# Two fused attention and feed-forward layers: softmax totals from a column of ones, intermediate results by tokens, later loads held back, more zero matmuls at the start

## The chip, the cores and the metric

The kernel runs on one core of a Trainium2 chip. The metric is the device time of one execution in microseconds (us), as the median of several runs; a profiled execution gives the trace beside it.

## What is computed

Two layers, each an attention branch `s` and a feed-forward branch `g` on the same layer-normalised input, joined as `x + s * silu(g)`. There are 4 batches of 1024 tokens, 128 features, all in float32.

```python
x = L0_attn_x                                   # (4, 1024, 128)
xn = layernorm(x)
s = L0_attn(xn)      # 16 heads of 8, window of 64 tokens back, ALiBi bias, softmax
g = silu(L0_ffn(xn)) # weights mixed from 8 experts, one mixture for each batch
x = x + s * g
xn = layernorm(x)
s = L1_attn(xn)      # attention over the 4 "batches" for each position, gated bias, Wo, bo
g = silu(L1_ffn(xn)) # silu(w1 x) * (w2 x), gelu(h1 .), gelu(h2 .), w3
return x + s * g
```

In the first attention the softmax divides each head's weighted values by the sum of its exponentials:

```python
score = jnp.einsum('bhqd,bhkd->bhqk', q, k) / scale + bias[None]
score = jnp.where(mask[None, None], score, -jnp.inf)
attn = jax.nn.softmax(score, axis=-1)
out = jnp.einsum('bhqk,bhkd->bhqd', attn, v)
```

## The kernel before

**Units and tiles.** A unit is 512 tokens of one batch, so there are 8 units, two to a batch. In the first attention a unit has 4 tiles of 128 queries. The second attention goes by 8 slices of 128 positions over all 4 batches, named by words with a star. Features lie on the partitions and tokens along the free axis nearly everywhere ("by features"); "by tokens" means the transpose of that.

**Order.** PE, DVE and ACT each run their queue in the order in which the program issues it (`manual_schedule`), and that order is written out as a string of words, `ORDER`: a letter for the step, a digit for the unit or batch and mostly one for the part. `s21` is the scores of unit 2, tile 1. The words name: l/n/k the layernorm before the first layer (statistics, scaling, transposing back), t the statistics of the middle one (its n and k have part 1), q the projections, m and v masked queries and values, s scores, b bias added, x exponential, o weighted values and totals, d division, A B C D the gate of the experts, E one expert added into the mixed weights (16 a batch), f and g the first feed-forward, r the residual on POOL, w h i j the second feed-forward. POOL and SP aren't held to the string; their instructions are placed by what they depend on, and each runs in order too.

**Scores and totals.** `scores` (L393) writes a tile's scores into a single PSUM buffer of four banks, `ps_S`; DVE adds the bias from there into SBUF (`biased`, L410), ACT takes the exponential in place (L741). `weighted` then makes, for the tile's 16 heads, the weighted values (L438: 32 products of 64 columns, weights of 32 columns taken from `vb`, which holds values in slots of 24 columns with 8 used) and the totals (L451: 16 products of 128 columns with a matrix of ones, `totals`, or its upper half where a batch's first keys are masked). Both fall into `ps_O`, features on partitions, so that the total stands at each of a head's 8 rows. `divided` (L462, L463) takes the reciprocal of 256 columns for a pair of tiles and multiplies.

**Feed-forward of the first layer.** `hid0` (L472) gives four blocks of hidden features. `out0` (L481) accumulates four products of 512 columns into one bank, mixed weights as the stationary operand, and ACT applies Silu with the bias of each feature (L485). `residual` (L490, L491) multiplies and adds on POOL. The middle layernorm needs tokens on partitions, so `ln_mid` (L224) transposes `x` four times a unit.

**Feed-forward of the second layer and output.** `gated` (L508 to L512), `hidden` (L520, L521; the heaviest group), `out1` (L531, L536, scaled by `w3s` in the Silu at L539). In the second attention's slices `project_out` (L666) is one product of 512 columns, `gated_out` (L672 to L675) adds the bias, multiplies with `g1`, adds `x` and stores. `last_batch` (L687 to L689) stores the last batch.

**Start and loads.** Three products with zeros (L266) run while the first loads come. A bound on the scores is worked out, and the program branches on it to one of two versions; the one with the running maximum left out (`exact` false) is taken. The first unit's expert tables go into buffers of the hidden blocks (`stream_first`, L339), those of later batches through three buffers `tw` (L294), issued when step A of the batch comes. Right after the branch SP issues all other loads: `x` twice (by features and, as `xt` into `g1`, by tokens), the second layer's weights (`load_l1`, L501) and `wa` (L693 to L699).

Of the kernel before, what the change touches and what calls it, by code (L numbers as in the profile page):

```python
# [29 lines left out]
C_ID, C_MP, C_SEL, C_EXP, C_TOT, C_TOF = np.cumsum([0, 128, 4, 64, 256, 128]).tolist()  # L30
C_N = C_TOF + 128
# [3 lines left out]
for _name, _n in (  # L35
    ("gb1", 1), ("gb2", 8), ("b1", 4), ("b2", 1), ("bq", 1), ("bk", 1), ("bv", 1), ("bo", 1),
    ("gW", 8), ("gb", 8), ("ga", 1), ("pb", 4), ("w1s", 4), ("w2s", 4), ("h1s", 4), ("h2s", 4), ("w3s", 1),
):
    VEC[_name] = (sum(n for _, n in VEC.values()), _n)
V_N = sum(n for _, n in VEC.values())  # L40


def constants():
# [13 lines left out]


    tot = np.tile((r[None, :] // 8 == g[:, None]).reshape(1, P), (P, 1))
    c[:, C_TOT:C_TOT + P] = tot  # L60
    c[:, C_TOF:C_TOF + P] = tot * (p[:, None] < W)
# [24 lines left out]

ORDER = """
    l1 n10
    q0 m03 m00 m01 z m02 s00 b00 k10 A00 A01 s01 B0 b01 v00 C0 D0 E0 v01 s02 v03 x01 E0 E0 v02 E0 E0 x00 b02
    o00 s03 E0 x02 E0 l3 E0 E0 b03 o01 E0 f0 d01 E0 f1 E0 x03 E0 f0 f0 E0 E0 f1 E0 l2 o02 o03 n30 f0 d03 n20  # L90
    g0 g0
    q1 v11 k20 k30 r0 t0 f1 m11 A10 n01 m12 g1 k01 v10 f1 v13 w0 m13 g1 m10 v12 w0 w0 s10 A11 b10 w0 s11 x10
    b11 x11 h0 h0 s12 o10 b12 o11 s13 b13 h0
    q2 d11 x12 h0 o12 B1 x13 C1 D1 E1 E1 E1 E1 i0 E1 o13 E1 d13 i0 E1 E1 i0 E1 E1 r1 i0 E1 E1 t1 E1 f2 E1 j0
    v20 v23 j0 f2 f2 E1 m21 m20 E1 n11 g2 v21 f2 k11 m22 g2 v22 w1 m23 w1 s20 w1 b20 w1 h1 l4 x20 h1 s21 n40
    o20 b21 x21 h1 o21 s22 d21 b22 h1 x22 l5 i1 i1 s23 b23 o22 x23 n50 i1 i1 o23 j1 j1 k50 f3 d23
    q3 r2 t2 m31 n21 f3 k40 f3 v31 f3 g3 m30 A20 k21 v32 v33 g3 w2 v30 w2 m32 m33 w2 A21 s30 b30 w2 x30 B2
    h2 s31 o30 b31 C2 x31 h2 s32 o31 D2 h2 E2 b32 h2 x32 E2 i2 d31 i2 E2 o32 E2 E2 E2 s33 E2 E2 b33 E2 x33
    E2 i2 E2 i2 E2 o33 E2 d33
    q4 f4 r3 E2 E2 m43 E2 f4 j2 v40 t3 n31 f4 m41 f4 j2 g4 k31 v42 m40 v43 g4 w3 w3 m42 l6 v41 w3 w3 s40 b40  # L100
    n60 h3 x40 h3 s41 b41 o40 k60 l7 n70 h3 x41 h3 k70 s42 o41 b42 i3 f5 i3 s43 b43 d41 x43 x42 i3 i3 o42
    o43 j3 d43 j3 r4
    q5 t4 f5 m53 f5 n41 A30 m51 m50 f5 v51 g5 k41 g5 v53 w4 m52 v52 v50 w4 w4 s50 b50 w4 x50 A31 h4 h4 B3
    o50 s51 b51 C3 x51 h4 D3 E3 E3 E3 s52 b52 E3 E3 E3 E3 o51 x52 h4 i4 d51 s53 b53 E3 E3 E3 E3 o52 x53 i4
    i4 E3 i4 o53 d53 E3 r5 j4 f6 E3 E3
    q6 f6 t5 m61 E3 f6 m63 f6 n51 v60 j4 v61 g6 k51 g6 v62 w5 m62 v63 w5 m60 w5 w5 s60 b60 h5 x60 h5 s61 o60
    b61 x61 h5 h5 o61 s62 i5 i5 b62 d61 x62 i5 s63 b63 x63 i5 o62 o63 d63 f7 r6 f7 j5 f7 t6 j5 n61 f7
    q7 k61 m71 m70 g7 v70 v73 v71 w6 m72 g7 m73 w6 v72 *A0 w6 s70 *B0 b70 *V0 w6 s71 b71 x70 h6 *A1 *b0 s72
    b72 x71 *C0 *E0 *B1 *N0 x72 o70 h6 *b1 *D0 o71 *A2 d71 *V1 *C1 *B2 o72 s73 *E1 *N1 h6 *G0 b73 *F0 *b2 h6
    *D1 x73 *C2 i6 *E2 o73 i6 *G1 d73 r7 *Y0 *A3 *N2 t7 *V2 *B3 *D2 *b3 n71 *V3 i6 i6 *C3 *E3 *F1 k71 j6 *N3  # L110
    *Y1 w7 *G2 *D3 j6 w7 w7 *A4 *F2 *G3 *F3 *Y2 *Y3 y60 *V5 *B4 *b4 *A5 *A6 w7 *V6 *V4 *C4 *B5 *E4 *b5 *V7
    h7 *B6 *A7 h7 *b6 *N4 *C5 *B7 *b7 *D4 h7 *C7 *E5 h7 *G4 *E7 *F4 *N5 *Y4 *D5 *G5 i7 *C6 *E6 *N6 i7 *F5
    *N7 *D6 *Y5 i7 *D7 *G6 i7 *F6 *G7 j7 *Y6 j7 *F7 y70 *Y7 y71
# [4 lines left out]
def block_kernel(ctx: ExitStack, tc: tile.TileContext, a: dict, out: bass.AP):  # L118
# [20 lines left out]

    x = main.tile([P, B, S], F32, tag="x", name="x")  # L140

    g1 = main.tile([P, B, S], F32, tag="g1", name="g1")
    xt = [g1[:, b, :].rearrange("p (i d) -> p i d", d=P) for b in range(B)]
# [7 lines left out]
    tb = const.tile([P, FC + 1, E], F32, tag="tb", name="tb")  # L151
# [6 lines left out]
    nc.scalar.dma_start(out=g1[:, 0, 0:U], in_=a["xt"][:, 0:U])  # L158
    nc.sync.dma_start(out=wqkv, in_=a["wqkv"])
    nc.sync.dma_start(out=cst, in_=a["const"])  # L160
    nc.scalar.dma_start(out=g1[:, 0, U:S], in_=a["xt"][:, U:S])
# [15 lines left out]
    totals = [cst[:, at:at + P].rearrange("p (g c) -> p g c", g=4) for at in (C_TOT, C_TOF)]  # L177
# [7 lines left out]
    DVE.memset(vb[:, 0:2328], 0.0)  # L185
    POOL.memset(vb[:, 2328:24 + 9 * 512], 0.0)
    slots = vb[:, 24:24 + 9 * 512].rearrange("p (m h q) -> p m h q", m=9, h=H)[:, :, :, 0:HD]

    def tokens(u):

        b, c = u // 2, (u % 2) * U
        return b, slice(c, c + U)

# [21 lines left out]
    def ln_in(u):  # L215

        return ln_stats(xt[u // 2][:, 4 * (u % 2):4 * (u % 2) + 4, :])

    def ln_mid(u):

        b, cx = tokens(u)
        turned = ps.tile([P, 4, P], F32, tag="O", name="ps_T")
        for i in range(4):
            PE.transpose(turned[:, i, :], x[:, b, cx.start + i * P:cx.start + (i + 1) * P], ident)  # L224
        return ln_stats(turned)
# [32 lines left out]

    one = const.tile([P, 1], F32, tag="one", name="one")
    POOL.memset(one, 1.0)  # L260
    in_order = {mybir.EngineType.PE, mybir.EngineType.Activation, mybir.EngineType.DVE}
    with tc.manual_schedule(engines=in_order | {mybir.EngineType.Pool}):
        steps = bound()

        for i in range(3):
            PE.matmul(bank(), lhsT=vb[:, 0:P], rhs=vb[:, 0:U], start=True, stop=True)  # L266
            if i == 1:
                next(steps)
        scale = ln_in(0)
        next(steps)  # L270
        fast = nc.values_load(flag[0:1, 0:1], min_val=0, max_val=1)
        ln_back(0, scale())

    def program(exact):
# [41 lines left out]
        def gates_c(b, gr):  # L316
            shares = small([P, FC + 1, E], "shares")
            DVE.tensor_tensor(shares, tb, gr.unsqueeze(1).to_broadcast([P, FC + 1, E]), ALU.mult)
            mb = at.tile([P, FC + 1], F32, tag="mb", name="mb", bufs=2)
            DVE.tensor_reduce(mb, shares, AX.X, ALU.add)  # L320
            DVE.tensor_tensor(mb, mb, v("b1", 0, FC + 1), ALU.add)
            own = [at.tile([P, F], F32, tag=f"mw{j}", name=f"mw{j}", bufs=2) for j in range(2)]
            mixed[b] = (own[0], own[1], mb)

# [27 lines left out]
        def qkv(u):  # L352
# [26 lines left out]
            def value(i):  # L379
                copy = DVE.tensor_copy if u else ACT.copy  # L380
                rows, first = ((slice(0, W), 0), (slice(0, W), 1), (slice(W, P), 1), (slice(W, P), 2))[i]
                copy(slots[rows, first:first + 7:2], src[rows])
# [45 lines left out]
        def weighted(u, t, pr):  # L428

            if t % 2 == 0:  # L430
                put(("op", u), ps.tile([P, 2, 2 * P], F32, tag="O", name="ps_O"))
            op = made["op", u][:, :, (t % 2) * P:(t % 2) * P + P]
            for i in range(2):
                qs = slice(W * i, W * i + W)
                at0 = 24 + 512 * (2 * t + i)
                for g in range(4):
                    for j in range(4):
                        PE.matmul(  # L438
                            op[32 * j:32 * j + 32, 0, qs],
                            lhsT=vb[:, at0 + 128 * j + 24 * g:at0 + 128 * j + 24 * g + 32],  # L440
                            rhs=pr[:, j, g, qs],
                            start=(g == 0),
                            stop=(g == 3),
                        )
            spans = ((slice(0, P), 0),)
            if u % 2 == 0 and t == 0:
                spans = ((slice(0, W), 1), (slice(W, P), 0))
            for qs, first in spans:
                for g in range(4):
                    for j in range(4):  # L450
                        PE.matmul(  # L451
                            op[32 * j:32 * j + 32, 1, qs],
                            lhsT=totals[first][:, g, :],
                            rhs=pr[:, j, g, qs],
                            start=(g == 0),
                            stop=(g == 3),
                        )

        def divided(t, op, s):

            inv = small([P, 2 * P], "inv")
            DVE.reciprocal(inv, op[:, 1, :])  # L462
            DVE.tensor_tensor(s[:, (t - 1) * P:(t + 1) * P], op[:, 0, :], inv, ALU.mult)  # L463
# [12 lines left out]
        def out0(u, hid):  # L476
            b, _ = tokens(u)
            _, m2, mb = mixed[b]
            op = bank()
            for c in range(FC):  # L480
                PE.matmul(op, lhsT=m2[:, c * P:(c + 1) * P], rhs=hid[:, c, :], start=(c == 0), stop=(c == FC - 1))  # L481
                if c == 1:
                    yield None
            g = tmp.tile([P, U], F32, tag="g", name="g", bufs=1)
            ACT.activation(g, op, AF.Silu, bias=mb[:, FC:FC + 1])  # L485
            yield g

        def residual(u, g, s):
            b, cx = tokens(u)
            POOL.tensor_tensor(g, g, s, ALU.mult)  # L490
            POOL.tensor_tensor(x[:, b, cx], x[:, b, cx], g, ALU.add)  # L491
# [6 lines left out]
        def load_l1():  # L498
# [376 lines left out]
```

## Time and profile before

| what | value |
|---|---|
| median of 3 runs | 586.19 us (586.15 to 586.88) |
| profiled execution, time | 588.99 us |
| profiled execution, span of the core | 587.1 us |
| mean granted TensorE clock | 0.984 |
| loads and stores | 29.35 MB, mean 50 GB/s |
| instruction packets of queue 8 | 46, 0.75 MB |

A profile's line of a group names the line in the kernel, the engine, the operation, the tile written and the tiles read, the shapes and the count; behind the first bar stand the busy time in us and the mean ns of one, behind the second the idle time of the engine just ahead, and what ended it. PE is a matmul, PEld the load of its stationary operand. A product in f32 appears as two passes, a transpose as one, so 32 products are 64 records. Rows of 40 digits are slices of 14.7 us, each digit tenths. In a timeline the columns are start, length, engine, line, operation, tiles, shapes and count, and in square brackets the engine's idle time before it. In a table by stretches each engine has its busy us and its count of instructions, then come granted clock, DMA share and GB/s.

### The profile page before, as it was taken

How to read it: one execution, taken by the hardware profiler on the slowest of the kernel's cores; microseconds unless marked ns; L12 is line 12 of the kernel's file. 1: busy time of each engine (PE TensorE's matmuls, PEld its weight loads, DVE VectorE, ACT ScalarE, POOL GpSimd, SP SyncE). 2: the span in 40 equal slices, each digit the busy share in tenths (PEclk: the TensorE clock that was granted, in tenths of full speed). 3: DMA queues.
4: the chain of work that ended last, by engine and by line, in shares of the span. 5: the costliest groups of instructions: out<-in, count | busy, mean ns of one | idle time of the engine just before them, and what ended most of it. 6: DMA issues, size and time to landing. Idle time of an engine off the chain costs nothing.

```text
span 587.1 us, 12660 instructions
## 1 busy us (share of the span) xinstructions
PE 564.8 (96%) x5608; PEld 287.5 (49%) x5608; DVE 333.9 (57%) x545; ACT 334.2 (57%) x380; POOL 110.6 (19%) x123
## 2 busy tenths in 40 slices
PE   6589999999999999999999999999999999999995
PEld 2356455535455454545554554445554555444443
DVE  5876535755333473663325384743146768878764
ACT  2546757286655736556566564664866747345441
POOL 3012000211002000211010000300021334557433
PEclk8869999999999999999999999999999999999999
DMA  8980000620000012400000032000000000001002
GB/s 306 400 343 2 2 2 3 213 74 2 1 2 0 1 52 95 145 2 1 1 2 1 1 109 73 0 1 2 2 2 1 2 2 11 5 27 33 1 15 64
DMA packets 10750, 29.35 MB, mean 50 GB/s; under 512 B 1216, under 2 KB 4800, under 8 KB 9664
## 3 DMA queue, kind: packets, MB, share of 16 engines
q1 hardware_dynamic: 10256, 26.90, 12.9%
q10 hardware_dynamic: 432, 1.57, 0.7%
q8 instruction: 46, 0.75, 0.5%
q14 instruction: 16, 0.13, 0.1%
HBM read 26.37 MB, written 2.10 MB: 48 GB/s over the span
## 4 chain that ended last, share of the span: by engine, by line
PE 93%; ACT 2%; DMA 1%; DVE 1%; issue 1%; POOL 0%; ACTq 0%; DVEq 0%
PE ps_M L520 38%; PE ps_O L438 6%; PE ps_S L393 6%; PE ps_O L451 5%; PE ps_M L481 5%; PE ps_M L508 4%; PE ps_M L472 4%; PE ps_M L509 4%; PE ps_M L536 4%; PE ps_M L569 4%; PE ps_S L648 1%; PE ps_M L617 1%; PE ps_M L231 1%; PE ps_S L364 1%; PE ps_S L361 1%
## 5 line engine op out<-in xcount | busy, mean ns | idle before, releaser
L520 PE MATMUL ps_M<-big,l1h 128*128 128x512 f32 x512 | 229.6, 598 | 0.0
L520 PEld LDWEIGHTS ps_M<-big,l1h 128*128 128x128 f32 x512 | 94.6, 190 | 115.1 <-issue 110.8
L410 DVE TENSOR_TENSOR big<-ps_S,bias 128x2048 f32<-128x2048 f32 x32 | 73.3, 2290 | 94.9 <-PE ps_S L393 78.0
L521 ACT ACTIVATE big<-ps_M,vec 128x512 f32<-128x512 f32 x64 | 43.9, 687 | 109.1 <-PE ps_M L520 108.7
L741 ACT ACTIVATE big<-big 128x2048 f32<-128x2048 f32 x32 | 61.0, 1910 | 15.4 <-DVE big L410 15.1
L462 DVE RECIPROCAL inv<-ps_O 128x256 f32<-128x256 f32 x16 | 28.1, 1754 | 37.0 <-PE ps_O L451 36.9
L521 ACT ACT_TABLE_LOAD x35 | 44.9, 1283 | 5.6 <-PE ps_M L520 5.0
L490 POOL TENSOR_TENSOR g<-g,s 128x512 f32<-128x512 f32 x8 | 10.8, 1353 | 184.1 <-DVE s L463 179.7
L512 DVE SCALAR_TENSOR_TENSOR big<-ps_M,vec,t2k 128x512 f32<-128x512 f32 x32 | 23.9, 748 | 32.6 <-PE ps_M L509 16.5
L438 PEld LDWEIGHTS ps_O<-big,vb 128*32 128x32 f32 x2048 | 32.3, 114 | 19.6 <-issue 15.0
L438 PE MATMUL ps_O<-big,vb 128*32 128x64 f32 x2048 | 37.5, 226 | 3.9 <-ACT big L741 3.4
L451 PE MATMUL ps_O<-big,cst 128*32 128x128 f32 (+1 forms) x1152 | 36.5, 269 | 3.2 <-issue 3.2
L393 PE MATMUL ps_S<-qm,k 32*64 32x256 f32 (+1 forms) x768 | 36.9, 472 | 2.5 <-DVE big L410 2.5
L330 DVE SCALAR_TENSOR_TENSOR mw<-tw,gr,mw 128x512 f32<-128x512 f32 x42 | 35.1, 836 | 1.2
L741 ACT ACT_TABLE_LOAD x26 | 33.4, 1283 | 3.3 <-DVE big L410 2.9
L508 PE MATMUL ps_M<-xn,l1w 128*128 128x512 f32 x64 | 33.4, 603 | 1.2 <-ACT g L485 1.2
L509 PE MATMUL ps_M<-xn,l1w 128*128 128x512 f32 x64 | 32.9, 595 | 0.0
L473 ACT ACTIVATE big<-ps_M,mb 128x512 f32<-128x512 f32 x32 | 21.7, 687 | 18.8 <-PE ps_M L472 18.5
L511 ACT ACTIVATE t2k<-ps_M,vec 128x512 f32<-128x512 f32 x32 | 22.0, 686 | 17.8 <-PE ps_M L508 17.3
L472 PE MATMUL ps_M<-xn,mw 128*128 128x512 f32 x64 | 31.2, 597 | 0.0
L451 PEld LDWEIGHTS ps_O<-big,cst 128*32 128x32 f32 x1152 | 29.3, 115 | 3.9 <-issue 3.8
L393 PEld LDWEIGHTS ps_S<-qm,k 32*64 32x64 f32 x768 | 18.9, 133 | 24.2 <-issue 11.0
(148 smaller groups left out, 687.0 us busy)
## 6 DMA issues: line engine op xcount, KB each, us to landing
tw<-in_tw SPq DMA_DIRECT2D x24, 512.0 KB, 4.1
big<-in_tw SPq DMA_DIRECT2D x4, 1024.0 KB, 8.2
l1h<-in_l1h SPq DMA_DIRECT2D x2, 1024.0 KB, 15.3
g<-in_xt SPq DMA_DIRECT2D x3, 512.0 KB, 12.1
x<-in_x SPq DMA_DIRECT2D x1, 1536.0 KB, 14.2
out<-t2k SPq DMA_DIRECT2D x8, 192.0 KB, 2.1
bias<-in_bias ACTq DMA_DIRECT2D x1, 1024.0 KB, 7.9
l1w<-in_l1w SPq DMA_DIRECT2D x3, 256.0 KB, 13.9
```

The source lines that it names most:

```text
L330: DVE.scalar_tensor_tensor(m, more[e // 2][:, e % 2, :], gr[:, e:e + 1], base if e == 0 else m, ALU.mult, ALU.add)
L393: PE.matmul(sp[rows, j, :, q0:q0 + n], lhsT=k[r, key:key + W], rhs=qm[r, :, t * P + q0:t * P + q0 + n], start=True, stop=True,)
L410: DVE.tensor_tensor(pr, sp, bias, ALU.add)
L438: PE.matmul(op[32 * j:32 * j + 32, 0, qs], lhsT=vb[:, at0 + 128 * j + 24 * g:at0 + 128 * j + 24 * g + 32], rhs=pr[:, j, g, qs], start=(g = ...
L451: PE.matmul(op[32 * j:32 * j + 32, 1, qs], lhsT=totals[first][:, g, :], rhs=pr[:, j, g, qs], start=(g == 0), stop=(g == 3),)
L472: PE.matmul(hp, lhsT=m1[:, c * P:(c + 1) * P], rhs=xn[:, b, cx], start=True, stop=True)
L481: PE.matmul(op, lhsT=m2[:, c * P:(c + 1) * P], rhs=hid[:, c, :], start=(c == 0), stop=(c == FC - 1))
L508: PE.matmul(p1, lhsT=wt["w1"][:, c * P:(c + 1) * P], rhs=xn[:, b, cx], start=True, stop=True)
L509: PE.matmul(p2, lhsT=wt["w2"][:, c * P:(c + 1) * P], rhs=xn[:, b, cx], start=True, stop=True)
L520: PE.matmul(hp, lhsT=wt[name][:, i, c * P:(c + 1) * P], rhs=hid[:, i, :], start=(i == 0), stop=(i == FC - 1))
L521: ACT.activation(new[:, c, :], hp, AF.Gelu, scale=v(name + "s", c))
L741: ACT.activation(pr, pr, AF.Exp)
```

## The change

1. **Totals.** The slots of `vb` get a ninth column, set to one once; `value` writes only the eight others. `weighted` takes the weights so that each product gives 8 values and the total of a head in 9 neighbouring rows; the three first head groups of a tile fall into one of two parts of `ps_O`, the fourth groups of both tiles share a third part. The second loop with `totals` goes, as do its constants. Where a batch's first keys are masked, the ninth column is zeroed with the rest of the slot.
2. **By tokens.** A new step c copies the pair's result from PSUM on ACT, p transposes its three parts on PE, and d divides by tokens: reciprocals of 24 and 8 columns, and two multiplications. `out0`, `out1` and `project_out` take the hidden block as the stationary operand and the weights as the moving one, four products of 128 columns for each of 512. Biases that lay on partitions are now rows: a new step H (`row_bias`) makes one product for each batch's bias row, DVE adds it ahead of the Silu; `bo` is added by DVE in a step of its own; `w3` is scaled once on POOL by `w3s` (step Z). `x` is loaded, kept and stored by tokens, so that `xt`, the transposes of `ln_mid` and one of two loads of `x` go.
3. **Loads.** `load` (steps L0, L1, L2) sets one column of its target on DVE and then issues the load; the words stand in the first unit's last third. Only `x[1]` is still issued right after the branch.
4. **Start.** Five zero products instead of three, behind a first memset of 512 columns; after the first transposes `row_weights` (two products) and one more zero product of 256 columns.
5. **Order.** The string of words is new throughout. The first unit before:

```
l1 n10 q0 m03 m00 m01 z m02 s00 b00 k10 A00 A01 s01 B0 b01 v00 C0 D0 E0 v01 s02 v03 x01 E0 E0 v02 E0 E0 x00 b02
o00 s03 E0 x02 E0 l3 E0 E0 b03 o01 E0 f0 d01 E0 f1 E0 x03 E0 f0 f0 E0 E0 f1 E0 l2 o02 o03 n30 f0 d03 n20 g0 g0 q1
```

and after:

```
l1 q0 n10 m03 m00 m01 z m02 s00 k10 A00 A01 b00 s01 B0 b01 v00 C0 H0 D0 v01 v03 E0 E0 E0 E0 x01 s02 b02 E0
E0 v02 l3 E0 x00 E0 o00 x02 E0 E0 s03 o01 b03 c01 E0 f1 p01 d01 E0 E0 f0 E0 L0 x03 E0 E0 f0 f0 l2 f1 o02
o03 c03 n30 f0 g0 n20 g0 L1 L2 k30 p03 d03 r0 q1
```

The diff, cut to its core:

```diff
-    DVE.memset(vb[:, 0:2328], 0.0)
+    DVE.memset(vb[:, 0:U], 0.0)
+    DVE.memset(vb[:, U:2328], 0.0)
     POOL.memset(vb[:, 2328:24 + 9 * 512], 0.0)
-    slots = vb[:, 24:24 + 9 * 512].rearrange("p (m h q) -> p m h q", m=9, h=H)[:, :, :, 0:HD]
+    slots = vb[:, 24:24 + 9 * 512].rearrange("p (m h q) -> p m h q", m=9, h=H)[:, :, :, 0:HD + 1]
...
-    def ln_mid(u):
-
-        b, cx = tokens(u)
-        turned = ps.tile([P, 4, P], F32, tag="O", name="ps_T")
-        for i in range(4):
-            PE.transpose(turned[:, i, :], x[:, b, cx.start + i * P:cx.start + (i + 1) * P], ident)
-        return ln_stats(turned)
+    def ln_of(u):
+        return ln_stats(by_tokens(x, u))
...
+    POOL.memset(slots[:, :, :, HD], 1.0)
+    def row_weights():
+
+        rp = bank((P, 4, P))
+        for i in range(2):
+            PE.matmul(rp[:, i, :], lhsT=sb[:, i * P:(i + 1) * P], rhs=sb[:, 2 * P:3 * P], start=True, stop=True)
+        DVE.tensor_scalar(wb[:, 0, :], rp[:, 0, :], 1.0 / S, None, ALU.mult)
+        DVE.tensor_copy(wb[:, 1, :], rp[:, 1, :])
...
-        for i in range(3):
-            PE.matmul(bank(), lhsT=vb[:, 0:P], rhs=vb[:, 0:U], start=True, stop=True)
-            if i == 1:
+        for i in range(5):
+            idle(vb, U)
+            if i == 2:
                 next(steps)
...
         ln_back(0, scale())
+        row_weights()
+        idle(vb, U // 2)
...
+        def row_bias(hrep):
+            rp = bank()
+            PE.matmul(rp[:, 0:D], lhsT=hrep, rhs=wb[:, 0, :], start=True, stop=True)
+            row = at.tile([P, D], F32, tag="row", name="row")
+            DVE.tensor_tensor(row, rp[:, 0:D], wb[:, 1, :], ALU.add)
+            return row
...
             if t % 2 == 0:
-                put(("op", u), ps.tile([P, 2, 2 * P], F32, tag="O", name="ps_O"))
-            op = made["op", u][:, :, (t % 2) * P:(t % 2) * P + P]
+                put(("op", u), ps.tile([P, 3, P], F32, tag="O", name="ps_O"))
+            op, odd = made["op", u], t % 2
             for i in range(2):
                 qs = slice(W * i, W * i + W)
                 at0 = 24 + 512 * (2 * t + i)
                 for g in range(4):
+                    part, row = (odd, 9 * g) if g < 3 else (2, 9 * odd)
                     for j in range(4):
+                        col = at0 + 128 * j + 32 * g - row
                         PE.matmul(
-                            op[32 * j:32 * j + 32, 0, qs],
-                            lhsT=vb[:, at0 + 128 * j + 24 * g:at0 + 128 * j + 24 * g + 32],
+                            op[32 * j:32 * j + 32, part, qs],
+                            lhsT=vb[:, col:col + 32],
                             rhs=pr[:, j, g, qs],
...
-                        PE.matmul(
-                            op[32 * j:32 * j + 32, 1, qs],
-                            lhsT=totals[first][:, g, :],
-                            rhs=pr[:, j, g, qs],
...
-            inv = small([P, 2 * P], "inv")
-            DVE.reciprocal(inv, op[:, 1, :])
-            DVE.tensor_tensor(s[:, (t - 1) * P:(t + 1) * P], op[:, 0, :], inv, ALU.mult)
+        def taken(u, op):
+
+            ab = tmp.tile([P, 3, P], F32, tag="ab", name="ab", bufs=1)
+            ACT.copy(ab, op)
+            return ab
+
+        def turned(ab):
+            tp = bank((P, 4, P))
+            for i in range(3):
+                PE.transpose(tp[:, i, :], ab[:, i, :], ident)
+            return tp
...
+            DVE.reciprocal(i3, most[:, :, :, HD])
+            DVE.reciprocal(i1, rest[:, :, :, HD])
...
-            op = bank()
+            op = bank((P, 4, D))
             for c in range(FC):
-                PE.matmul(op, lhsT=m2[:, c * P:(c + 1) * P], rhs=hid[:, c, :], start=(c == 0), stop=(c == FC - 1))
+                for i in range(4):
+                    PE.matmul(op[:, i, :], lhsT=hid[:, c, i * P:(i + 1) * P], rhs=m2[:, c * D:(c + 1) * D], start=(c + i == 0), stop=(c + i == FC + 2))
...
-            ACT.activation(g, op, AF.Silu, bias=mb[:, FC:FC + 1])
+            DVE.tensor_tensor(g, op, made["row", b].unsqueeze(1).to_broadcast([P, 4, D]), ALU.add)
+            ACT.activation(g, g, AF.Silu)
...
+        def load(*names):
...
+                DVE.memset(to[:, 0:1], 0.0)
+                nc.sync.dma_start(out=to, in_=of)
...
-                op = st["op"] = spare((P, B, L))
-                PE.matmul(op, lhsT=wa[:, 3 * D:4 * D], rhs=xn[:, :, cx], start=True, stop=True)
+                op = st["op"] = spare((P, B, D))
+                for t in range(B):
+                    PE.matmul(op[:, t, :], lhsT=xn[:, t, cx], rhs=wa[:, 3 * D:4 * D], start=True, stop=True)
...
-                DVE.scalar_tensor_tensor(y, op[:, 0:n, :], v("bo"), g1[:, 0:n, cx], ALU.add, ALU.mult)
-                DVE.tensor_scalar(xn[:, n, cx], op[:, n, :], v("bo"), None, ALU.add)
+                DVE.tensor_tensor(xn[:, :, cx], op, v("bo", 0, D).unsqueeze(1).to_broadcast([P, B, D]), ALU.add)
+                DVE.tensor_tensor(y, xn[:, 0:n, cx], g1[:, 0:n, cx], ALU.mult)
...
-        nc.sync.dma_start(out=g1[:, 1, :], in_=a["xt"][:, S:2 * S])
-        nc.sync.dma_start(out=x[:, 0, :], in_=a["x"][:, 0:S])
-        load_l1()
-        for b in range(2, B):
-            nc.sync.dma_start(out=g1[:, b, :], in_=a["xt"][:, b * S:(b + 1) * S])
-        nc.sync.dma_start(out=x[:, 1:B, :].rearrange("p b s -> p (b s)"), in_=a["x"][:, S:B * S])
-        nc.sync.dma_start(out=wa, in_=a["wa"])
+        nc.sync.dma_start(out=x[:, 1, :], in_=a["x"][:, S:2 * S])
...
+            "L": lambda i: load(*(("w1", "w2", "h1"), ("h2", "w3"), ("wa", "x"))[i]), "0": lambda n: idle(cst, P * n), "y": lambda u, i: last_batch(u, i, U if u < 7 else U // 2),
```

## The prediction

> **What bounds the kernel now.** I read the page's first two parts, then a table by stretches, the groups by line, the chain of waits, and the timeline of the first unit and of the end.
>
> ```profile
> PE 564.8 (96%) x5608; PEld 287.5 (49%) x5608; DVE 333.9 (57%) x545; ACT 334.2 (57%) x380; POOL 110.6 (19%) x123
> ...
> PEclk8869999999999999999999999999999999999999
> DMA  8980000620000012400000032000000000001002
> ```
>
> PE is the only engine near its span, and it is short of clock only in the first three slices, where the DMA engines are full. The table by stretches (length, then busy time of PE, PEld, DVE, ACT, POOL, granted clock, DMA share) separates two regimes:
>
> ```profile
> 15.00:30.00 15.00, 9.11 (x184) 5.99 (x186) 12.35 (x20) 8.56 (x13) 1.41 (x4) 0.84 1.00 400
> 30.00:45.00 15.00, 12.14 (x226) 7.61 (x221) 11.32 (x20) 6.67 (x6) 1.95 (x2) 0.71 0.79 319
> ...
> 250.00:300.00 50.00, 50.00 (x548) 25.39 (x551) 20.97 (x39) 33.08 (x35) 3.06 (x6) 1.00 0.01 2
> ```
>
> From about 45 us on, PE works without a gap at full clock, and DVE and ACT are half idle: there a PE pass removed is time removed, and other engines' work is free as long as PE has other work queued. Before 45 us DVE is the fullest queue and PE waits at half clock.
>
> PE's busy time counts overlapping passes twice, so I price passes from start to start. Chain of waits (start, length), then timeline of the second unit:
>
> ```profile
> 143.68 1.03 PE ps_O L438 x64
> 144.71 0.89 PE ps_O L451 x64
> 145.60 3.63 PE ps_M L520 x8
> ```
> ```profile
> 49.32 3.60 PE L481 MATMUL ps_M<-big,mw 128*128 128x512 f32 x8
> ...
> 52.75 1.02 PE L361 MATMUL ps_S<-xn,wqkv 128*128 128x512 f32 x2
> ...
> 54.47 1.05 PE L364 MATMUL ps_S<-wqkv,xn 128*128 128x128 f32 x8
> ...
> 55.36 1.04 PE L231 MATMUL ps_M<-cst,nt 128*128 128x128 f32 x8
> ```
>
> The totals (L451) of one 128-token tile take 0.89 us after its values (L438, 1.03 us). A 512-column f32 product is two passes, (52.75 - 49.32) / 8 = 0.429 us each. A 128-column pass with weights of its own each time is (55.36 - 54.47) / 8 = 0.111 us: four of them are 0.444, so turning a product round into four by tokens costs only 0.015 us a pass.
>
> The first unit, in the timeline: the first bias addition, PE standing in the middle of the totals, and (above) the second unit's queries at 52.75.
>
> ```profile
> 16.96 2.29 DVE L410 TENSOR_TENSOR big<-ps_S,bias 128x2048 f32<-128x2048 f32 x1 [1.31 <-PE ps_S L393]
> ...
> 33.24 0.65 PE L451 MATMUL ps_O<-big,cst 128*32 128x64 f32 x15 [2.47 <-issue]
> ...
> 42.06 4.68 DVE L330 SCALAR_TENSOR_TENSOR mw<-big,gr,mw 128x512 f32<-128x512 f32 x6
> ```
>
> DVE's last expert step ends at 46.74, and DVE sat idle for 30 - 12.35 - 11.32 = 6.3 us between 15 and 45. The 2.47 us wait is for nothing the kernel does[...].
>
> [...]
>
> **The change part by part**, against the profiled execution (span 587.1, 1.9 around it, 589.0 in all; the median of the three runs, 586.2, is 0.5% lower, so a difference in us carries over).
>
> *Totals by a column of ones.* L451 goes. After the first unit that is 28 tiles at 0.89 = -24.9 us (up to 28 if a group followed by another one is worth the 1.0 us that such pairs take). L438 keeps its 32 products a tile, at other addresses: nothing. Added: the result is copied by ACT (16 copies; 582 ns for 512 columns at L232, so about 0.45, 7 us in all, beside PE), turned by three transposes per pair of tiles, and divided by tokens. 42 transposes after the first unit, against 32 that the middle layernorm no longer needs because x now lies by tokens: 10 more at 0.12 = +1.2, and some 7 more changes between tiled and whole array at 0.11 = +0.8. DVE's division falls from 1.75 + 0.42 to about 1.05: from 553 ns for 64 reciprocals (L637) and 1754 for 256 the cost is 0.15 + 0.0063 each, so 0.30 + 0.20, and two small multiplications of 0.35 + 0.2 (256 take 0.42). It is used where DVE waits for PE anyway; free but in the first unit. New is the way o, copy, turn, divide, residual, layernorm: a copy behind an exponential (1.91) and a table load (1.28) on ACT can arrive 3 us late. The order puts other steps between; I take +1.0 in all, bounds -1 (the new order may also remove small gaps: PE is idle 2.3 us between 45 and 575) and +9.
>
> *By tokens.* Passes that were 512 wide: out0 8 in each of 7 later units, out1 8 in each of 7 (the last unit's are halves already), output projection 2 in each of 8 slices: 128 x 0.015 = +1.9. The row bias is two more passes for each of 3 later batches, 0.11 each: +0.7. On DVE 8 additions of 0.69 (a 512-column PSUM read, L372) before the Silu and about 0.35 more per slice in the output step, hidden by PE except in the last slice. DVE's sum falls to about 322 us. w3's scaling is one POOL step of about 1.4 us, long before use.
>
> *Loads held back, fewer bytes.* x no longer comes twice: 2.1 MB less. After the first unit's weights only x[1] and three of the next batch's tables (stream of A10, issued by SP ahead of L0) follow; w1, w2, h1 wait for a DVE memset in the middle of the expert steps, h2, w3, wa and x[2:4] for one after the first output product. So the queues are empty from about 24 us, by (2.6 + 4.2 + 0.5 + 1.6 MB) / 400 GB/s, to 38[...]. SP stands behind those memsets, but what is queued there (the fourth table of batch 1) also waits for a buffer until E1, near 100 us. The loads return as 4.2 MB between 38 and 52 us, when PE has become the bound[...]. Bounds 0 and 2.5 (the stall seen); I take +0.5. w1 is needed about 10 us after its issue and takes 4: hidden.
>
> *More zero matmuls, first unit.* A shorter first memset (512 of 2328 columns, about 0.45 of 2.0 us) lets PE start near 1.8 rather than 3.3, and five zero products instead of three, then the row weights and a half one, fill PE to 11 us; so the projections, 1.65 + 1.71 + 1.18 us at half clock in the chain, should run in about 2.6. The first bias addition then comes at about 15.6 instead of 16.96 (it is held by the four masks on ACT, 2.4 us, and the layernorm before it). From there DVE's queue to the last expert step is 4 x 2.29 + 16 x 0.76 + one layernorm's statistics 1.2 + six small steps 1.2 + a division 1.05 + memsets 0.3 = 25.1, and one wait of about 1 for the second scores (single ps_S buffer): 41.7. PE's products of out0 (32 x 0.111 = 3.6), four transposes and three more (0.8) follow: the second unit's queries start at about 46.2 instead of 52.75, -6.5. Bounds: -8.5 (exponentials earlier) and -3 (clock still lost while PE waits for exponentials near 25 us, with both output groups slow).
>
> *End.* The last slice's output is two DVE steps before POOL instead of one: +0.4.
>
> Sum: -24.9 + 1.2 + 0.8 + 1.0 + 1.9 + 0.7 + 0.5 - 6.5 + 0.4 = -24.9. From the median: 586.2 - 24.9 = **561.3**, said as 561.
>
> **Rivals.** *Loads of weights bind the products by tokens* (slower). 256 + 256 + 64 = 576 passes get weights of 128 columns each. If a pass took as long as its load, 190 ns, that is 576 x 0.079 = +45.5 us: 606. It decides from 0.111 + 24.9 / 576 = 0.154 us a pass. For it: PEld's mean of 190 ns. Against: the eight L364 passes at 111 ns, same shapes.
>
> *The first unit doesn't shorten* and the late loads stall PE once: 561.3 + 5 + 2 = about 568. For it: exponentials and scores through one PSUM buffer still alternate, and PE idles there as before. Against: DVE's own sum above.
>
> *The longer way to the middle layernorm leaves PE without work* for about 1.5 us in each of 7 units: 571. For it: ACT's table loads of 1.28 us and banks in threes. Against: the units are interleaved, and PE's stretches of second-FFN products are 14 us long.
>
> *More is saved*: totals at 1.0 a tile, first unit -8.5, no new waits: 586.2 - 31.5 = 554.7. For it: pairs of tiles at 4.05 us. That the totals aren't really gone is ruled out by the instruction order: no product has the ones matrix any more.
>
> **Numbers.** Forecast 561 (own range 557 to 565): 0.62. More saved: 0.14. First unit not shorter: 0.14. Waits: 0.07. Weight loads: 0.03. From 553 to 569 the first three cases and most of the fourth's lower part lie inside. About 0.2% is what a measurement of this kernel can tell from no change; faster 0.96, same 0.01, slower 0.03.
>
> **What would show it.** Passes of out0 and out1 start 0.11 us apart (0.19: the weight-load rival). Values of a tile, no totals: about 1.0 us to the next group. Queries of the second unit at about 46 us. PE busy in every stretch of 50 us from 50 to 550 at 49 or more; gaps named by ACT's copy or DVE's division would be the third rival. No PE wait named issue before 38 us. The forecast is wrong if PE's gaps after 50 us sum to over 8 us or the second unit starts after 50.

## The result and the profile after

The changed kernel takes 566.87 us (median of 4 runs, 566.34 to 566.92) against 586.27 for the kernel before on the same chip: ratio 0.9665, 95% interval 0.9648 to 0.9682, 19.4 us less. Run again for the experiments, on another chip, it took 566.5 against 588.22: ratio 0.9636 (0.9615 to 0.9657). The kernel before scatters more than the three runs ahead of the prediction showed: 39 runs on one chip lay between 585.4 and 590.6. The forecast was 561, the range 553 to 569.

The profiled execution took 566.92, its span is 565.1. The page after, busy times and slices:

```profile
PE 541.8 (96%) x4914; PEld 299.1 (53%) x4914; DVE 323.9 (57%) x599; ACT 332.5 (59%) x391; POOL 113.6 (20%) x125
...
PEclk9989999999999999999999999999999999999998
DMA  7908001610000033200000041000000000000002
```

PE lost 23 us of busy time and is still the bound. DVE came to 323.9 (estimated: 322). The DMA engines are now idle in the third slice and busy in the fourth, where the held loads lie. The table by stretches after (length, busy PE, PEld, DVE, ACT, POOL, clock, DMA share, GB/s):

```profile
30.00:45.00 15.00, 13.09 (x292) 7.81 (x282) 14.78 (x38) 11.84 (x13) 2.39 (x3) 0.90 0.08 20
...
250.00:300.00 50.00, 50.00 (x494) 29.07 (x493) 16.09 (x43) 33.92 (x38) 5.40 (x7) 1.00 0.00 1
```

DVE works 14.78 of 15 us between 30 and 45, where it worked 11.32 (13.97 in a second profile of the kernel before, below); later PE is nearly without a gap, as before: its gaps from 50 us on sum to 3.5 us, 2.2 before. The chain of waits, now with nothing between a tile's values and other work:

```profile
155.28 1.03 PE ps_O L457 x64
156.31 7.06 PE ps_M L560 x16
```

The timeline of the start and of the first unit after:

```profile
3.40 0.34 POOL L254 MEMSET vb<- 128x144 f32 x1 [0.60 <-DVE vb L185]
...
3.80 5.42 PE L267 MATMUL ps_M<-vb 128*128 128x512 f32 x6 [3.80 <-POOL vb L254]
...
9.15 0.22 PE L243 MATMUL ps_M<-nrm,one 128*1 128x32 f32 x2
...
10.01 0.14 DVE L251 TENSOR_SCALAR flag<-fm 1x1 int32<-1x1 f32 x1
...
18.84 2.29 DVE L426 TENSOR_TENSOR big<-ps_S,bias 128x2048 f32<-128x2048 f32 x1 [0.81 <-PE ps_M L226]
...
44.40 3.73 PE L511 MATMUL ps_M<-mw,big 128*128 128x128 f32 x32
...
47.97 0.60 PE L226 MATMUL ps_M<-cst,nt 128*128 128x128 f32 x4
...
48.73 1.02 PE L377 MATMUL ps_S<-xn,wqkv 128*128 128x512 f32 x2
```

Three things stand here. The first zero product waited until 3.80 us, for POOL: the column of ones lies inside the stretch of `vb` that the zero products read, so they wait for the step that writes it (and aren't quite zero). The bound's product sat behind six passes of them, so that the flag on which everything branches came at 10.01 us, 2.1 later than before. And out0 by tokens takes (47.97 - 44.40) / 32 = 0.112 us a pass. The second unit's queries start at 48.73, 4.0 us earlier than before; I had said 46.2.

Splitting both spans at the second unit's queries and at the last output projection's first pass (579.53 before, 556.51 after):

| stretch | before | after | difference |
|---|---|---|---|
| start to second unit's queries | 52.75 | 48.73 | -4.0 |
| to the last output projection | 526.78 | 507.78 | -19.0 |
| to the end | 7.55 | 8.61 | +1.1 |

The middle one, by what PE's passes take from start to start (their lengths overlap: a pass of L520 before lasts 598 ns, and 24 of them in a row take 10.50 us): totals -28.0, values +2.1 (their last pass now has the change to another shape that the totals had), middle layernorm's transposes -3.6, transposes of the new way +6.1, out1 +1.5, row bias +1.4, out0 +0.9, layernorm back +0.9, other groups together -0.2. The 0.9 of the layernorm is mostly one wait of this execution (0.77 us at 57.2); in the changed kernel's second profile (below) the group takes 7.1 us as before, and the middle stretch 506.92.

### The profile page after: what moved, and what is told of

It is laid out like the page before. It is cut to its first block, busy times and chain, and to the rows that moved or that the text cites. A ratio compares the mean times of both kernels' runs of the same rounds, so it can differ in the third digit from the quotient of the medians.

```text
span 565.1 us, 11348 instructions
## 1 busy us (share of the span) xinstructions
PE 541.8 (96%) x4914; PEld 299.1 (53%) x4914; DVE 323.9 (57%) x599; ACT 332.5 (59%) x391; POOL 113.6 (20%) x125
## 4 chain that ended last, share of the span: by engine, by line
PE 86%; DVE 8%; ACT 3%; POOL 1%; issue 1%; ACTq 0%; POOLq 0%; DVEq 0%
PE ps_M L560 38%; PE ps_S L409 6%; PE ps_O L457 5%; PE ps_M L548 5%; PE ps_M L549 5%; PE ps_M L511 5%; PE ps_M L500 4%; PE ps_M L573 4%; PE ps_M L606 3%; PE ps_M L267 1%; PE ps_S L685 1%; PE ps_M L226 1%; PE ps_M L654 1%; DVE mw L346 1%; PE ps_M L474 1%
## 5 line engine op out<-in xcount | busy, mean ns | idle before, releaser
L484 DVE RECIPROCAL inv<-ps_M 128x24 f32<-128x24 f32 x16 | 4.9, 306 | 63.2 <-PE ps_M L474 63.1
L457 PEld LDWEIGHTS ps_O<-big,vb 128*32 128x32 f32 x2048 | 30.9, 112 | 18.8 <-issue 17.0
L457 PE MATMUL ps_O<-big,vb 128*32 128x64 f32 x2048 | 35.1, 223 | 3.4 <-ACT big L770 3.4
L573 PEld LDWEIGHTS ps_M<-l1w,big 128*128 128x128 f32 x256 | 30.5, 192 | 4.7 <-issue 3.9
L511 PEld LDWEIGHTS ps_M<-mw,big 128*128 128x128 f32 x256 | 30.3, 192 | 4.4 <-issue 3.0
L573 PE MATMUL ps_M<-l1w,big 128*128 128x128 f32 x256 | 31.2, 276 | 0.0
L511 PE MATMUL ps_M<-mw,big 128*128 128x128 f32 x256 | 30.9, 275 | 0.0
```

The lines of the kernel that those rows point to most:

```text
L457: PE.matmul(op[32 * j:32 * j + 32, part, qs], lhsT=vb[:, col:col + 32], rhs=pr[:, j, g, qs], start=(odd + i + g == 0), stop=(odd + i + g = ...
L511: PE.matmul(op[:, i, :], lhsT=hid[:, c, i * P:(i + 1) * P], rhs=m2[:, c * D:(c + 1) * D], start=(c + i == 0), stop=(c + i == FC + 2))
L573: PE.matmul(op[:, k, :], lhsT=hid[:, i, at0:at0 + P], rhs=wt["w3"][:, i, :], start=(i + k == 0), stop=(i + k == FC + n - 2))
```

## The experiments

**The kernel before once more.** No edit.

> The kernel before, unchanged, profiled a second time. Its first profiled execution took 588.99 us, 2.8 over the median of 586.2, and lay at half clock from 11.5 to 14.9 us while PE made the first projections[...]. Theory: the 2.8 us are in the first 50 us of that one execution[...], so this one shows a span of about 584.3, a time of about 586.2, and the second unit's queries at about 50 instead of 52.75. Rival: a profiled execution of this kernel is always 2.8 us longer, and this one shows about 587 and 589 again. The times without a profile: 586.2 for both theories.

587.06 us (20 runs, 586.01 to 589.05), ratio 1.0001 (0.9987 to 1.0015). The profiled execution took 588.45, its span is 586.5, with the first projections at 0.43 to 0.47 us a pass (granted clock 1.00 in the first 15 us, 0.89 in the first profile) and the second unit's queries at 52.07. Neither theory holds. The span isn't 584.3. The rival's 587 and 589 nearly came, but this execution lies 1.4 us over its median, not 2.8, and the same kernel gives 586.0 and 589.05 without any change, so the 2.8 us are best read as scatter. Part of it can be named: the first bias addition comes at 15.95 here, at 16.96 where the first projections took 0.72 to 0.86 us a pass. The chain of waits of this execution (start, length, what):

```profile
33.33 1.63 issue
...
41.99 2.36 issue
```

Waits of PE for nothing that the profile shows come back, at other moments than the 2.47 us at 30.8 seen before. What PE waits for in them isn't shown. In the first profile it resumes, at 33.24 and 39.44 us, 1.3 and 1.4 us after the end of a 16 KB packet of queue 8, which the page names instruction; the two packets took 1.03 and 1.07 us. That full queues cause such waits was my estimate, and the longest one speaks against it: from 41.99 to 44.35 it passes with the queues all but empty (DMA share 0.14 and 0.00, in the columns of the tables by stretches):

```profile
42.00:43.00 1.00, 0.00 (x0) 0.00 (x0) 1.00 (x6) 0.99 (x2) 0.00 (x0) 1.00 0.14 57
43.00:44.00 1.00, 0.00 (x0) 0.00 (x0) 1.00 (x9) 1.00 (x3) 0.51 (x2) 1.00 0.00 0
```

**Totals alone.** In the kernel before, `weighted` ends after the values:

```diff
-            spans = ((slice(0, P), 0),)
...
-                            lhsT=totals[first][:, g, :],
...
-            DVE.reciprocal(inv, op[:, 1, :])
+            DVE.reciprocal(inv, op[:, 0, :])
```

> The kernel before with the products that form the totals left out (the second loop of weighted); the division takes the reciprocal of the values instead, so the result isn't a softmax. Nothing else changes. Theory (PE bound, a tile's totals cost 0.9 to 1.0 us): 28 tiles after the first unit give 25 to 28 us, the first unit some 2 more: 557 to 560 us. Rival (the time is set by DVE or ACT behind PE, and the saving is partly given back as waits): 565 or more.

558.42 us against 586.81, ratio 0.9511 (0.9488 to 0.9534): -28.4. Its second unit's queries come at 45.46 (52.07 in the kernel before run with it), and from there to the last output projection it takes 502.91 us against 526.67: -23.8, that is 0.85 a tile. The whole is as expected and PE time really is time, but the parts aren't: 23.8 in the later units (25 to 28 expected) and 6.6 in the first (2 expected), counted from an execution of the kernel before that holds 4 us of PE's waits named issue. That the changed kernel wins 7 to 9 us less than this must be what the rest of the change costs, if the parts add up.

**Products by tokens alone**, in the kernel before; out0 as example:

```diff
-                PE.matmul(op, lhsT=m2[:, c * P:(c + 1) * P], rhs=hid[:, c, :], start=(c == 0), stop=(c == FC - 1))
+                for i in range(4):
+                    PE.matmul(op[:, i * P:(i + 1) * P], lhsT=hid[:, c, i * P:(i + 1) * P], rhs=m2[:, c * P:(c + 1) * P], start=(c + i == 0), stop=(c + i == FC + 2))
```

> The kernel before with out0, out1 and the output projection turned into products by tokens, the hidden block as the stationary operand, four of 128 columns for each of 512; the results then lie in an order that the rest doesn't expect. Theory (a pass costs 0.111 us, its load of weights is hidden): about 64 + 56 + 16 passes of 512 dearer by 0.015 us each, +2 us: 588 us. Rival (the load of 190 ns binds the pass): +40 us or more, 626 us.

588.76 us, ratio 1.0032 (1.0024 to 1.0040): +1.9. The timeline:

```profile
48.38 3.73 PE L482 MATMUL ps_M<-mw,big 128*128 128x128 f32 x32
51.95 1.02 PE L361 MATMUL ps_S<-xn,wqkv 128*128 128x512 f32 x2
```

32 passes in 3.57 us, 0.112 us each, as in the forecast, while one load of weights takes 0.19; the rival in which loads of weights bind the pass is out. That the +1.9 meets the forecast is in part luck: from the second unit's queries to the last output projection this profile takes 527.19 us against 526.67 in the second profile of the kernel before, only 0.5 more. The turned groups take 2.2 us more there, and values and totals 1.4 less, mostly because waits of PE near 300 and 425 us aren't there. The rest of the medians' difference isn't located.

**The changed kernel once more**, as base of the next three. No edit.

> The changed kernel unchanged, on the chip on which the variants of its start and its loads run, as their base: 566.9 us, second unit's queries near 48.7 us in the profile.

566.5 us (565.29 to 567.74), ratio 0.9636 (0.9615 to 0.9657); profiled 565.29. Its zero products also start at 3.80, but the bound's product comes at 7.99, not 9.15, since fewer of them ran at 0.85 us a pass (the six take 4.26 us instead of 5.42); the queries come at 47.76. From there to the last output projection it takes 506.92 us, 0.9 less than in the first profile of the changed kernel.

**Zero products that don't wait for the ones**, the half product at the end too.

```diff
-    DVE.memset(vb[:, 0:U], 0.0)
-    DVE.memset(vb[:, U:2328], 0.0)
+    DVE.memset(g1[:, 0, 0:U], 0.0)
+    DVE.memset(vb[:, 0:2328], 0.0)
...
-            idle(vb, U)
+            idle(g1[:, 0, :], U)
```

> The changed kernel with the zero products reading a zeroed stretch of g1 instead of vb, so that they don't wait for the column of ones that POOL writes into vb (PE's first product stood until 3.80 us). Theory (the wait of the zero products for the ones, and of the bound's product behind three of them, delays the flag, the branch and all of the first unit): PE starts near 1.5, the flag comes about 2.3 us earlier, and so do the second unit's queries, near 46.4: 564.6 us. Rival (the first unit is set by DVE's queue and the loads, and the start has slack): unchanged, 566.5 to 567.

564.71 us (563.84 to 564.79), ratio 0.9599 (0.9579 to 0.9618), 1.8 below the base. The timeline:

```profile
1.44 5.49 PE L267 MATMUL ps_M<-g 128*128 128x512 f32 x6 [1.44 <-DVE g L184]
...
6.86 0.27 PE L243 MATMUL ps_M<-nrm,one 128*1 128x32 f32 x2
...
16.48 2.29 DVE L426 TENSOR_TENSOR big<-ps_S,bias 128x2048 f32<-128x2048 f32 x1 [0.81 <-PE ps_M L226]
```

The queries come at 46.38. The start is on the path. That the queries now come where the prediction had put them (46.2) is luck in part: the first bias addition is still 0.9 later than its 15.6, and the way from there 0.7 shorter.

**The bound's product earlier.**

```diff
-        for i in range(5):
+        for i in range(3):
             idle(vb, U)
-            if i == 2:
+            if i == 0:
```

> The changed kernel with three zero products instead of five, and the bound's product after the first of them instead of after the third; the zero products still wait for the ones. Theory (the flag waits for three zero products at half clock): the flag comes about 2.5 us earlier (near 7.5), and the second unit's queries near 46.5, if the clock holds: 564.5 us. Rival (what the two more zero products buy in clock is worth more): PE falls to half clock for the first projections, and the time is 566.5 or more.

564.36 us, ratio 0.9598 (0.9579 to 0.9616). The flag comes at 6.79, the first projections at 11.55 and at 0.43 to 0.47 us a pass, the queries at 46.76. Taking the bound out from behind the zero products does the same as starting them earlier.

**Loads early again**, in the changed kernel:

```diff
-                DVE.memset(to[:, 0:1], 0.0)
...
+        load("w1", "w2", "h1", "h2", "w3", "wa", "x")
...
-            "L": lambda i: load(*(("w1", "w2", "h1"), ("h2", "w3"), ("wa", "x"))[i]),
+            "L": lambda i: None,
```

> The changed kernel with all later loads issued right after the branch, without the memsets, as before the change. Theory[...]: +1 to +2.5 us[...], 568 to 569 us, with a wait named issue between 24 and 40 us. Rival (DVE sets the first unit, such a wait has slack): 566.5 to 567. Rival the other way (loads held back collide with PE's later work): under 566.

567.35 us (566.92 to 567.58), ratio 0.965 (0.9631 to 0.9668): 0.9 above the base, with overlapping intervals, so this doesn't settle between no effect and one of the lower bound. Its profile has no wait of PE named issue in the first 50 us, at a DMA share of 1.02 between 15 and 30; the wait expected between 24 and 40 us isn't there. From the first bias addition to the second unit's queries it takes 30.66 us (29.89 and 30.09 in the two profiles of the changed kernel), and one expert step on DVE takes 1.48 us instead of 0.75; why, wasn't tried.

**Loads held back in the kernel before.** The wait in question is the one of 2.47 us of PE at 30.8 in its first profile. The same memsets and loads, in the old order of words:

```diff
-        load_l1()
...
-    o00 s03 E0 x02 E0 l3 E0 E0 b03 o01 E0 f0 d01 E0 f1 E0 x03 E0 f0 f0 E0 E0 f1 E0 l2 o02 o03 n30 f0 d03 n20
+    o00 s03 E0 x02 E0 l3 E0 E0 b03 o01 E0 f0 d01 E0 f1 E0 L0 x03 E0 f0 f0 E0 E0 f1 E0 l2 o02 o03 n30 f0 d03 n20
...
-    g0 g0
+    g0 g0 L1 L2
```

> The kernel before with its later loads (the second layer's weights, two batches of x by tokens, three of x by features, wa) held back by memsets on DVE at the places that the changed kernel has: one set in the last third of the first unit, the other after its output products. Theory[...]: that wait goes and the time falls by 2 to 3 us, ratio about 0.996. Rival (the wait has slack, or comes back where the loads now lie): within 0.1% of the kernel before.

583.25 us against 586.71, ratio 0.994 (0.9922 to 0.9958): -3.5, above the expected 2 to 3. The table by stretches, of the kernel before (second profile) and of this one:

```profile
30.00:45.00 15.00, 11.01 (x280) 7.08 (x277) 13.97 (x33) 9.59 (x10) 3.22 (x4) 0.96 0.79 319
```
```profile
30.00:45.00 15.00, 14.02 (x329) 8.86 (x329) 14.81 (x36) 10.45 (x12) 3.22 (x4) 0.99 0.32 108
```

With the DMA share down from 0.79 to 0.32 PE works 3 us more in the stretch; of its waits named issue one of 0.89 us is left (3.99 in the two above). The queries come at 47.11 instead of 52.07, and the middle stretch is the same (526.62 and 526.67), so all of the gain is in the first unit. Of these 5.0 us about 3 are the waits; another 1.6 lie behind the 2.36 us wait, where PE's granted clock falls to 0.50 and the totals of a tile take 2.02 us instead of 1.09. By the medians the held loads are worth 3.5 us in the old order and 0.9, not told apart from nothing, in the new one. Why they differ wasn't tried.

**The new way's own cost**, c and p left out of the changed kernel, and the two reciprocals replaced by copies:

```diff
-            "s": score, "b": bias_add, "x": power, "o": weigh, "c": take, "p": turn, "d": divide,
+            "s": score, "b": bias_add, "x": power, "o": weigh, "c": lambda u, t: None, "p": lambda u, t: None, "d": divide,
...
-            divided(t, made["tp", u, t], once(
+            divided(t, made["op", u], once(
```

> The changed kernel without the copy on ACT and the three transposes of each pair of tiles; the division reads the weighted values' PSUM tile as it lies, with copies in place of the two reciprocals, so the result isn't the softmax. Theory (the new way costs PE its 48 transposes and nothing else): -6 to -7 us from the changed kernel, about 560. Rival (the way over ACT also leaves PE waiting): -8 or more, under 558.5. Rival the other way (the time isn't PE's): -3 or less.

559.78 us, ratio 0.9543 (0.9524 to 0.9563), 6.7 to 7.1 below the changed kernel's two medians (5.5 to 7.2 by the ratios, as the three were taken on different chips). The transposes take 6.1 us of PE in the middle stretch and 0.7 in the first unit. The copy on ACT and the longer way therefore cost little beside them: in the profile after, PE waits 1.01 us for a division and 0.24 for a copy after 50 us. The third rival, with 1.5 us in each of seven units, is out.

**No zero products.**

```diff
-            idle(vb, U)
+            pass
...
         row_weights()
-        idle(vb, U // 2)
```

> The changed kernel without any zero products, the row weights still in their place. Theory A (zero products win by the clock: the first projections would run at half clock, 1.7 us longer, and the gain from an earlier flag, some 2.3 us, is partly given back): 565 to 566.5 us. Theory B (they cost more than they bring, since the flag waits for them): 564.5 us or less. Theory C (the clock is lost for the whole first unit): 568 or more.

564.91 us, ratio 0.962 (0.9602 to 0.9637), between theories A and B. The timeline shows both effects:

```profile
10.71 2.08 PE L376 MATMUL ps_M<-xn,wqkv 128*128 128x512 f32 x2
12.58 1.91 PE L377 MATMUL ps_M<-xn,wqkv 128*128 128x512 f32 x2
14.28 1.73 PE L379 MATMUL ps_V<-wqkv,xn 128*128 128x128 f32 x8
```

The projections start 3.1 us earlier than in the profile after (13.84) and need 5.2 us until the scores start instead of 3.6, at half speed (0.94 us a pass instead of 0.47). As the change places them, the zero products gain nothing: 564.9 without, 566.5 and 566.9 with. By the ratios (0.962; 0.9636 and 0.9665) the loss is clear of noise against the first comparison, not against the second.

**Another start.** Zero products from `g1` as above, four of them, the bound's product behind two, row weights after the first projections, no half product:

```diff
-        for i in range(5):
-            idle(vb, U)
-            if i == 2:
+        for i in range(4):
+            idle(g1[:, 0, :], U)
+            if i == 1:
...
-        row_weights()
-        idle(vb, U // 2)
...
-    q0 n10 m03 m00 m01 z m02
+    q0 n10 m03 m00 m01 z R m02
```

> The changed kernel with its start mended, meant to beat both: zero products read a zeroed stretch of g1, so they don't wait for the ones; the bound's product stands behind two of them and two follow; the row weights are made after the first projections, and the last half zero product is gone. Theory (each of these sat on the way to the first projections): they start near 10.9 instead of 12.7 to 13.8 us, and the time is about 2.5 to 3 us below the changed kernel, 563.8 or a ratio of 0.959. Rival (the clock is lost without the half zero product): 565 or more.

563.32 us (562.75 to 563.83), ratio 0.9597 (0.958 to 0.9614). The projections start at 10.29 and take 0.43 to 0.47 us a pass, the queries come at 45.60. It is the fastest by median of the variants that still compute the whole, 3.2 to 3.6 us under the changed kernel (2.3 to 4.0 by the ratios); from the two other starts (0.9599 and 0.9598) its ratio can't be told apart.

## Why the prediction was right, and where it was off

The sum said -24.9 us; measured were -19.4 in the first comparison and -21.7 in the second, and -22.0 between the two profiled spans. The mechanism held: a bound PE, and passes removed as time removed. That the parts came so near is luck in part, as the terms show.

- *Totals, products by tokens, new way*: my terms for the middle stretch sum to -18.8 (all but the first unit and the end); the profiles give -19.0, and -19.8 between the second profiles of both kernels. Singly: the values and totals -26.0 (taken: -24.9, with 0.8 for changes of shape counted apart), transposes +2.5 net (taken: +1.2), out0, out1 and the projection +2.9 (taken: +1.9), row bias +1.4 (taken: 0.7). The price of a tile was right: in most tiles values and totals take 0.92 and 0.99 us from start to start before, values alone 1.03 after, which makes 0.87 a tile and 24.4 for 28. The 0.8 was not, because one group of each tile is followed by another shape before and after; and about 1.4 us more went with waits of PE named issue beside the totals (near 85, 300 and 425 us). The gaps of PE from 50 us on grew by 0.4 to 1.4 us (taken: +1.0). The sum is closer than its terms, since they err both ways. Two stretches of 50 us stay under the 49 us of busy PE that the forecast named, 50 to 100 with 48.84 and 450 to 500 with 48.78.
- *Start*: the step that failed. The prediction put the first bias addition at 15.6 instead of 16.96, because "a shorter first memset ... lets PE start near 1.8 rather than 3.3". It came at 18.84. Two things were overlooked, both to be read in the diff and the order of instructions: the memset of ones overlaps the zero products' operand, and the bound's product went from behind two zero products to behind three, whose passes take 0.85 us. That is a term of -1.3 which was +1.9; the runs with each of the two put right bring back about 2 us. The base was off too: in the four other profiles with the old start the first bias addition comes at 15.71 to 15.95, so that most of the 1.3 us hoped for was there already, whenever the projections took 0.43 to 0.47 us a pass and not 0.72 to 0.86.
- *First unit from there*: 15.6 to 46.2 was 30.6 us in the prediction, 18.84 to 48.73 is 29.9. The sum of DVE's queue was the right thing to add up: 26.1 us with its wait to the end of the last expert step in the prediction, 25.0 in the profile.
- *Loads held back*: PE's waits named issue are there again in later profiles of the kernel before (1.63 and 2.36 us in the second), and holding the loads back is worth 3.5 us in the old order; in the new one 0.9 is measured, not told apart from nothing, so no separate gain of this change is shown on top of the shorter first unit. That they come from full queues was my estimate and isn't shown: the first profile has one of 0.34 us near 425 us at a DMA share of 0.00, and the second profile the one of 2.36 us, most of it with empty queues. The 0.5 us taken for the late loads rested on that estimate too; a stall of up to 2.5 us where they now lie isn't in the profile after: PE was busy 14.08 of 15 us from 45 to 60, and its two longest gaps there, 0.15 and 0.77 us, stand ahead of layernorm transposes and end with DVE's scaling.
- *End*: +1.1 instead of +0.4. The last loop's output takes 4.15 us from the projection to the last store's issue instead of 3.92, and the rest of the difference lies behind that issue (4.5 us to the end of the span, 3.6 before). What of it is the store itself wasn't tried.
- *The base*: I subtracted from a median of three runs and took the profiled execution's 2.8 us above it as a constant; the later runs show some 3 us of scatter, and 5 on one chip.

The single effects don't add up to the whole: -28.4 (totals), -3.5 (loads), +1.9 (tokens) and +6.9 (the new way, less 3.6 for the old transposes) +2 (start), +1.4 (row bias) and +1.1 (end) give -22.2, against -19.4 and -21.7 measured. The totals' and the loads' gains probably overlap in the first unit, where each shortens the same stretch (6.6 and 5.0 us of the queries' start); whether that is all of the remaining 0.5 to 2.8 us wasn't tried apart.

## What to carry to other kernels

Where one engine works without a gap, price its instructions from start to start in a stretch where they follow each other, and add them up: that sum came within 0.2 to 1 us of the 19.0 to 19.8 saved in a stretch of 508, though single terms were up to 1.9 us off and partly cancelled. A start is another matter: there every instruction queued ahead of the one that opens the way counts, zero products too (here six passes of 0.85 us), and a step that writes into the operand of such a filler makes it wait (here until 3.80 us). Before counting on a filler, look what it reads, who writes that last, and what stands behind it.

## What the runs showed of the hardware

- PE has waits for nothing that the profile shows: 2.47 and 0.39 us in the first unit of the first profile of the kernel before, 1.63 and 2.36 in the second, 0.89 with held loads. In the first profile PE resumes from both 1.3 and 1.4 us after the end of a 16 KB packet of queue 8; that they are waits for these packets isn't shown. A DMA share of 1.02 between 15 and 30 us came without such a wait (the loads early in the changed kernel), and at 0.00 one went on (the 2.36 us one).
- Behind the 2.36 us wait the granted clock fell to 0.50 (45 to 47 us), behind the 1.63 us one it stayed at 1.00 (35 to 37 us).
- A reciprocal on DVE took 306 ns for 24 columns (L484 after), 553 for 64 (L637 before) and 1754 for 256 (L462 before).
- A tile's group of tiled products took PE 0.11 to 0.12 us more where a group of another shape followed than where tiled products followed: totals 0.99 and 0.87 us from start to start, values 1.03 and 0.92.
- Zero products ahead of the product that opens the way delayed it by more than they brought here: in the profile after they ran at 0.85 us a pass (5.42 us for six), and with two fewer of them and the product after the first the kernel takes 564.36 us instead of 566.5.
